# Turning y between the tiles of the norm, weights made early, a final reduce moved ahead and filler products in TensorE's waits

## The chip, the cores and the metric

The kernel runs on one core of a Trainium2 chip. The metric is device time in microseconds of one execution, lower is better. The core has TensorE (PE; its weight loads are shown apart as PEld), VectorE (DVE), ScalarE (ACT), GpSimd (POOL) and SyncE (SP), which here only issues DMA transfers. All engines run their own queue of instructions in order and wait for one another through semaphores. Sixteen DMA engines carry the transfers.

## The reference

The input x is (4, 64, 64, 96): four images, 96 channels. Each image passes a convolution layer with a selective scan, an attention layer and a feed-forward layer, each added to its input; the first works on a group norm (32 groups of three channels over the image). Cut to what matters here:

```python
xz = bilinear(x, W_in, s_in, b_in)            # signs of both operands, 96 -> 384
xp, z = jnp.split(xz, 2, axis=-1)
t = conv3x3(sign(xp + move0), sc * sign(conv_W))   # 192 channels
t = prelu(t + conv_b + rp_b0) + rp_b1 + xp
u = silu(t)                                   # (4, 192, 4096)
# four directions k: rows, columns, and both reversed
dt, B, C = split(bilinear(u_k, Wl, sl, bl));  delta = softplus(bilinear(dt, Wd, sd, bd) + dt_bias)
h = exp(delta * A) * h + delta * u_k * B      # 16 states for each of 192 channels, along 4096 steps
y_k = sum(C * h) + D * u_k
y = y_0 + flip(y_2) + turned(y_1) + turned(flip(y_3))
y = layernorm(y) * ln_w + ln_b;  x = x + bilinear(y * silu(z), W_out, s_out, b_out)
# then linear attention (6 heads, q (k^T v)), and a feed-forward layer in 8-bit floats
```

"Turned" means that rows and columns of the 64 x 64 image are swapped.

## The kernel before

**The scan.** The work is cut into 1536 pieces: 4 images (b) times 4 directions (e, in the order k = 1, 3, 0, 2) times 4 chunks of 1024 steps (ci) times 6 groups of 32 channels (g) times 4 sets of 4 states (q). A piece is a tile of 128 rows (32 channels by 4 states) by 1024 steps. For piece i, `Scans.run` issues in this order: `loads` (broadcasts of B, C and delta, 512 KB each, on SP), `load_sums`, `carry` (the last column of a scan kept for the next chunk, ACT, L1597), `decay` for piece i+1 (exp(delta A) on ACT, L1554), `evacuate` (finished sums of y from PSUM, ACT, L1642), `reduce` for piece i-4 (the sum over states on PE, L1628 and L1633), `inject` for piece i+3 (w = delta u times B, on POOL, recorded at L443), `late_product` and `scan`. The scan itself is one DVE instruction of about 2.3 us; its product with C goes to DVE (1.23 us) or to POOL (2.35 us). Which of them is decided by two running tallies, `c.vec.us` and `c.gps.us`: POOL takes the product if DVE would be later than POOL, and the lead that one has over the other is carried to the next piece, up to 8. All tallied instructions of DVE and POOL carry the line L443.

**What runs beside it.** After each piece, `run` takes one step of the generators in `lanes` (the deltas of later chunks: `prepare`) and one step of `back`. The generator `back` works through everything that is not the scan: the prologues of the next images (projection, convolution, row stage), `turn(c, b)`, and the `Epilogue` of each image, `sums` (norm, gate and output projection of eight tiles of 512 positions), `middle` (the matrix of the attention) and `last` (attention and feed-forward). `turn` takes y of directions 1 and 3, which were scanned by columns, back to rows: sixteen loads yt on SP, sixteen copies yh on ACT (L1015, 96 x 512), and two stores. Direction 2 adds the turned y, so ahead of a piece of direction k = 2 the loop steps `back` until the turn is done:

```python
while KORD[self.pieces[i][1]] == 2 and self.pieces[i][0] not in c.turned:
    next(back)
```

In the kernel before, `back` comes to `turn(c, b+1)` after the sums of image b, or after the last tiles of image b-1. For the third image (b=2) it is this loop that forces it, at pieces 1056 to 1058.

**The head.** Before the first scan, `weights()` makes all constants (signs and transposes of the weights: winT, cwA and cwB, wR for the projection to dt, B and C, wdt, wdz and wdy for delta, sbR its scales, al and anm the decays, woutT and the small ones tpw and tpd). It is a lane that alternates with `prologue(0)`, which has a form of its own for the first image (`alone`): group norm, then `alone_parts`, the convolution in sixteen parts (two halves of 96 channels by eight tiles), and, as the parts leave room, the projection of later tiles (ix and iz, L647 and L648; tp and sz on ACT, L653 and L665). Per part PE makes the products cv (L745), DVE v (L783), ACT r (L784), two or three steps of e (L758, L759, L767) and the sign sg (L722). The signs go out as xg by POOL's queue (L730), a copy ut turned by POOL (L711) goes to memory as utd, and u as ud, by delayed stores on SP (`Later`, L462). Then comes the row stage: xa and xb (L874), their copies xr (L879), the projection acc (L940), tbc (L917) stored as bcd (L952) and the signs sgn (L920) stored as sgd (L953). The signs come back as g (L965), are transposed (gp, L975; gT, L982) and give the first deltas in `start`: dA_s (L1688), two steps w_s and w_d on DVE, and the broadcasts dl_s (L1711). `first_u` loads w_u (L1658, L1660), and `first_loads` loads the eight bc tiles of the first pieces, all on SP.

**The tail.** After the last scan `run` issues `next(back)`, then the last four reduces and the last evacuation (ys). Three lanes then finish the last image's sums: the epilogue's own lane, which has been working beside the scans, and two more (names ln0 and ln1) whose tiles need the last y. A fourth lane (l4) joins for `last`, so eight tiles are done in two rounds of four. In `norm` (products by `mm`, L1143), the form with `alone` set has the mean from PE and subtracts, scales, shifts and gates on DVE; the other form centers by the products yc and scales by the products sy on PE, and has one DVE step g for each half.

Of the kernel before, what the change touches and what calls it, by code (L numbers as in the profile page):

```python
# [25 lines left out]
CH = 1024  # L26
# [27 lines left out]
def hybrid_kernel(ctx: ExitStack, tc: tile.TileContext, a: dict, out: bass.AP):  # L54
# [108 lines left out]
    def weights():  # L163
# [39 lines left out]

        wi = temp("wi", [128, 3, DM], F32)
# [19 lines left out]
        wl = [temp(f"wl{o}", [128, DN], F32) for o in range(2)]  # L224
        for o in range(2):
            nc.gpsimd.memset(wl[o], 0.0)
            for kk in range(2):
                k, r0 = o + 2 * kk, 64 * kk
                nc.sync.dma_start(wl[o][r0 : r0 + 32, :], a["wl_bc"][32 * k : 32 * k + 32, :])
                nc.sync.dma_start(wl[o][r0 + 32 : r0 + 32 + NR, :], a["wl_dt"][k])  # L230
        wd = [temp(f"wd{x}", [128, NK, NR], F32) for x in range(2)]
        nc.sync.dma_start(wd[0], a["wd"][0:128])
        for r0 in (0, 64):
            nc.sync.dma_start(wd[1][r0 : r0 + 64], a["wd"][128:DN])
        wo = temp("wo", [DM, DN], F32)
        nc.sync.dma_start(wo, a["w_out"])
        small = {}
# [22 lines left out]
        nc.vector.tensor_tensor(sbx, pvx[:, :, B_X], pvx[:, :, MOVE0], ALU.add)  # L260
        wim = negmean("wim", wi, DM)
        wis = temp("wis", [128, 3, DM], BF16)
        for t in range(3):
            nc.scalar.activation(wis[:, t, :], wi[:, t, :], AF.Sign, bias=wim[:, t : t + 1])
        ps = transposed(winT, [wis[:, t, :] for t in range(3)])
        for x in range(2):
            nc.vector.tensor_copy(winB[:, 64 * x : 64 * x + 64], ps[0:DM, 128:DN], saturate=False)
        yield
        for i, cut in enumerate(cuts):
            nc.scalar.activation(cwA.rearrange("p t d -> p (t d)")[:, cut], cfa[i], AF.Sign, saturate=False)  # L270
            nc.scalar.activation(cwB[:, lines[i]], cfb[i], AF.Sign, saturate=False)
        yield

        part = temp("part", [96, 2, 2])
        for i in range(2):
            for h in range(2):
                nc.vector.tensor_reduce(part[:, h, i : i + 1], cwn[h][i], AX.X, ALU.add, apply_absolute_value=True)
            yield
# [108 lines left out]
        for name, dst in (("w1", w1q), ("w2", w2q), ("b1", b1q), ("b2", b2q)):  # L387
            q = dst if dst.dtype == F8 else temp(name + "q", list(dst.shape), F8)
            nc.vector.tensor_copy(q, small[name], saturate=False)
            if q is not dst:  # L390
                nc.vector.tensor_copy(dst, q)
# [1448 lines left out]
```

## Time and profile before

| what | us |
|---|---|
| median of three runs | 5361.95 (5360.22 to 5364.72) |
| the profiled execution, and its span | 5356.94, 5355.2 |
| busy: DVE, POOL, ACT, PE | 5004.4, 4951.9, 3606.7, 3387.5 |
| start to first scan | 180.2 |
| first scan to the end of the last | 5055.1 |
| last scan to the end | 120 |

The profile is of one execution. Times are in microseconds, an instruction's name is output<-inputs by the program's names, and L443 and the like are lines of the kernel. In answers in order of time, a line has the start, the duration, the engine, the line and operation, and in square brackets how long the engine was idle before it and what it had waited for last. Lines with an engine's name and q (SPq) are issues of transfers, whose duration is that of the issue alone. In answers by stretch, a line has the stretch, its length, the busy time of PE, PEld, DVE, ACT and POOL, and then the granted clock of TensorE (1 is full), the busy share of the DMA engines and GB/s.

### The profile page before, as it was taken

Reading aid. Unit: us, or ns where it says so; the run is one execution under the profiler, and the core shown is the slowest. Engines: PE = TensorE matmul, PEld = TensorE weight load, DVE = VectorE, ACT = ScalarE, POOL = GpSimd, SP = SyncE. Lnnn points to the kernel's source line nnn. Section 1 sums busy time; section 2 is a strip of 40 time slices with the busy share of each in tenths; the row PEclk is TensorE's granted clock in tenths of the full one; section 3 lists DMA queues with packets and bytes.
Section 4 is the critical chain, followed back from the end, with each engine's and each line's share of the span. In section 5 each row is a group of like instructions: output and inputs, shape, how many; then the busy total and the mean of one; then the engine's idle time right before and its main releaser. Section 6 shows DMA issues by size and latency. Waiting matters only on the chain. (4 is left out here: it accounts for less than half of the span.)

```text
span 5355.2 us, 61897 instructions
## 1 busy us (share of the span) xinstructions
PE 3387.5 (63%) x20029; PEld 1351.6 (25%) x20029; DVE 5004.4 (93%) x3168; ACT 3606.7 (67%) x5644; POOL 4951.9 (92%) x2254
## 2 busy tenths in 40 slices
PE   7457665567645666566676556775666676664577
PEld 3212222122222222222222222222222222221223
DVE  4699999999999999999999999997999999999995
ACT  6577767687766666677777766666776666776554
POOL 4699999999999999999999999998999999999990
PEclk8667776678866877677777768776777776676788
DMA  5666666867766666766666666666666566667652
GB/s 107 189 194 197 212 189 203 260 203 211 222 195 182 205 218 203 230 208 204 216 204 193 193 207 224 195 198 222 201 204 211 189 209 202 200 190 233 217 177 65
DMA packets 605594, 1068.83 MB, mean 200 GB/s; under 512 B 219771, under 2 KB 336916, under 8 KB 603540
## 3 DMA queue, kind: packets, MB, share of 16 engines
q1 hardware_dynamic: 602884, 1063.93, 63.7%
q8 instruction: 157, 2.57, 0.2%
q14 instruction: 169, 1.38, 0.1%
q0 software_dynamic: 1536, 0.79, 0.1%
q10 hardware_dynamic: 848, 0.15, 0.0%
HBM read 829.69 MB, written 228.30 MB: 198 GB/s over the span
## 5 line engine op out<-in xcount | busy, mean ns | idle before, releaser
L443 POOL TENSOR_TENSOR w<-dl,bc 128x1024 f32<-128x1024 f32 x1524 | 3549.5, 2355 | 60.3 <-PE yp L1628 43.7
L1554 ACT ACTIVATE dA<-dl,anm 128x1024 f32<-128x1024 f32 x1524 | 1701.3, 1116 | 511.9 <-DVE w L443 319.0
L443 DVE TENSOR_TENSOR_SCAN dA<-dA,cy,w 128x1024 f32<-128x1024 f32 x726 | 1700.7, 2343 | 61.3 <-ACT dA L1554 50.1
L443 POOL TENSOR_TENSOR w<-h,bc 128x1024 f32<-128x1024 f32 x570 | 1341.4, 2353 | 100.5 <-DVE h L443 95.5
L1628 PE MATMUL yp<-w,sum 128*32 128x256 f32 x12288 | 1230.4, 500 | 157.4 <-ACT pd L1508 109.4
L443 DVE TENSOR_TENSOR w<-dA,bc 128x1024 f32<-128x1024 f32 x966 | 1183.3, 1225 | 63.8 <-DMA bc<-bcd 1.9
L443 DVE TENSOR_TENSOR_SCAN h<-dA,cy,w 128x1024 f32<-128x1024 f32 x426 | 996.8, 2340 | 3.4 <-ACT dA L1554 3.1
L1597 ACT COPY cy<-dA 128x1 f32<-128x1 f32 x723 | 114.2, 158 | 829.1 <-DVE w L443 828.1
L1628 PEld LDWEIGHTS yp<-w,sum 128*32 128x32 f32 x12288 | 320.0, 127 | 1218.4 <-issue 741.0
L443 DVE TENSOR_TENSOR_SCAN dA<-dA,w 128x1024 f32<-128x1024 f32 x240 | 547.7, 2282 | 50.8 <-ACT dA L1554 48.2
L443 DVE TENSOR_TENSOR_SCAN h<-dA,w 128x1024 f32<-128x1024 f32 x144 | 328.1, 2279 | 9.0 <-POOL w L443 8.6
L1489 PE MATMUL dps<-gT,wdz 128*128 128x64 fp8e5 x1008 | 115.5, 314 | 323.8 <-ACT ys L1642 313.8
L1502 PE MATMUL dps<-sp,ident 128*128 128x512 f32 x378 | 266.4, 793 | 73.1 <-ACT dps L1498 72.7
L1633 PE MATMUL yp<-ya,back 128*128 128x256 f32 x576 | 225.6, 511 | 0.0
L1489 PEld LDWEIGHTS <-wdz 128*128 128x128 fp8e5 x1008 | 94.5, 152 | 402.2 <-issue 401.3
L806 PE MATMUL cv<-tp,cwA 128*96 128x512 fp8e5 x432 | 160.2, 492 | 43.1 <-ACT r L838 41.8
L1597 ACT COPY cy<-h 128x1 f32<-128x1 f32 x429 | 79.9, 186 | 158.9 <-DVE h L443 158.6
L1489 PE MATMUL dps<-gT,wdy 128*128 128x64 fp8e5 x504 | 57.0, 312 | 183.1 <-ACT ys L1642 182.8
L1280 PE MATMUL kv<-wkv,tt 97*128 97x192 f32 x240 | 76.8, 491 | 136.9 <-DVE tt L443 136.9
L1494 ACT ACTIVATE pd<-dps,dbias,pvd 128x512 f32<-128x512 f32 x189 | 144.0, 762 | 20.9 <-PE dps L1489 20.6
L1143 PE MATMUL yc<-eys,mean 96*96 96x512 f32 x240 | 133.5, 708 | 35.6 <-DVE vks L443 21.4
L1633 PEld LDWEIGHTS yp<-ya,back 128*128 128x128 f32 x576 | 118.9, 238 | 119.3 <-issue 88.6
(380 smaller groups left out, 4559.2 us busy)
## 6 DMA issues: line engine op xcount, KB each, us to landing
dl<-dld SPq DMA_DIRECT2D x762, 512.0 KB
bc<-bcd SPq DMA_DIRECT2D x512, 512.0 KB
dld<-pd SPq DMA_DIRECT2D x126, 512.0 KB
yd<-ys SPq DMA_DIRECT2D x764, 64.0 KB
dld<-pd SPq DMA_DIRECT2D x126, 256.0 KB
ya<-yd SPq DMA_DIRECT2D x192, 128.0 KB
pu<-ud SPq DMA_DIRECT2D x32, 512.0 KB
pu<-utd SPq DMA_DIRECT2D x31, 512.0 KB
```

The source lines that it names most:

```text
L443: return getattr(self.eng, name)(out, *args, **kw)
L806: nc.tensor.matmul(ps, w[:, 96 * h : 96 * h + 96], tp[:, 8 * q + dy : 8 * q + dy + 8, dx : dx + IW], start=(w is taps[0][1]), stop=(w is t ...
L1143: self.c.nc.tensor.matmul(ps, w, x, start=(i == 0), stop=(i == len(pairs) - 1))
L1280: nc.tensor.matmul(pk[i // 2][:, i % 2], tt[:, 128 * i : 128 * i + 128], c.wkv, start=True, stop=True)
L1489: nc.tensor.matmul(pv[:, s], wd[:, k, s], gT[:, :, c0 : c0 + 16], start=(s == 0), stop=(s == 7))
L1494: nc.scalar.activation(d[:, 0], ps, AF.Abs, scale=sc, bias=bi)
L1502: nc.tensor.matmul(ps, c.ident, t, start=False, stop=True, skip_group_check=True)
L1554: c.nc.scalar.activation(t, self.dlt[i // NQ][0], AF.Exp, scale=c.anm[:, g, NQ * KORD[e] + q : NQ * KORD[e] + q + 1])
L1597: self.c.nc.scalar.copy(self.carries[g, q], h[:, CH - 1 : CH])
L1628: c.nc.tensor.matmul(y[32 * x : 32 * x + 32, g % 2, :], c.sum4, prod[:, 256 * x : 256 * x + 256], start=(q == 0), stop=(q == NQ - 1 and no ...
L1633: c.nc.tensor.matmul(y[:, g % 2, :], w, src, start=False, stop=(n == len(more) - 1))
```

## The change

- `turn(c, b+1)` may now start between two tiles of `sums` or of `last` of image b, as soon as directions 1 and 3 of the next image are scanned (`between`); `back` leaves it out if it was done.
- After the last piece `run` makes no step of `back`, so the last four reduces come first; the tile that the third lane then works on takes the `alone` form of `norm`, with DVE in place of some products on PE.
- `keep_busy` issues products whose result is not used: 8 small ones ahead of the group norm's sums (csum), 24 after the last part of the convolution, 20 after the first image's row stage, and 15 in `middle` and in the first tile of `last` of the last image.
- The loads of wl and wd go to ACT's queue at the start, al is loaded with them; wR and wdt are made before the convolution starts, sbR and al early in it. woutT, tpw and tpd wait until the projection of the first image is over (`c.projected`). wdy's sixteen transfers, `first_u` and the eight first bc loads go to POOL's queue; the bc loads come right after `first_u`, one half of bcd's stores after the signs' stores or after the transposes. `clear_signs` moves ahead of the row stage for the first image.
- The tallies are set to zero after `start`.

```diff
@@ -201,6 +201,17 @@
             nc.vector.tensor_copy(dst, ps[:f, 0:at], saturate=False if dst.dtype == F8 else None)
             return ps

+        wl = [temp(f"wl{o}", [128, DN], F32) for o in range(2)]
+        for o in range(2):
+            nc.gpsimd.memset(wl[o], 0.0)
+            for kk in range(2):
+                k, r0 = o + 2 * kk, 64 * kk
+                nc.scalar.dma_start(wl[o][r0 : r0 + 32, :], a["wl_bc"][32 * k : 32 * k + 32, :])
+                nc.scalar.dma_start(wl[o][r0 + 32 : r0 + 32 + NR, :], a["wl_dt"][k])
+        wd = [temp(f"wd{x}", [128, NK, NR], F32) for x in range(2)]
+        nc.scalar.dma_start(wd[0], a["wd"][0:128])
+        for r0 in (0, 64):
+            nc.scalar.dma_start(wd[1][r0 : r0 + 64], a["wd"][128:DN])
...
-        wo = temp("wo", [DM, DN], F32)
+        wo, al = temp("wo", [DM, DN], F32), temp("al", [128, 2, NK * NS])
         nc.sync.dma_start(wo, a["w_out"])
+        nc.sync.dma_start(al, a["al"].rearrange("p h k s -> p h (k s)"))
         small = {}
...
-            yield
-        nc.vector.tensor_tensor(csc, part[:, :, 0], part[:, :, 1], ALU.add)
-        nc.vector.tensor_scalar(csc, csc, 1.0 / (9 * DN), None, ALU.mult)
-
-        nc.vector.tensor_tensor(cbias, pv[:, :, CONV_B], pv[:, :, RP0], ALU.add)
...
+            nc.scalar.activation(cwB[:, lines[i]], cfb[i], AF.Sign, saturate=False)
+        wdt = [temp(f"wdt{x}", [NR, NK * 32]) for x in range(2)]
+        for x, t in enumerate(wds):
+            transposed(wdt[x].bitcast(F8), [t[:, k, :] for k in range(NK)])
+        yield
...
+            yield
+            if i == 0:
+                for o in range(2):
+                    transposed(wR[:, o].rearrange("p x m -> p (x m)"), [wes[o][:, x, :] for x in range(4)])
+                yield
...
         for r0 in (0, 64):
             for s in range(8):
                 at = r0 + NR * s
-                nc.sync.dma_start(wdy.bitcast(F32)[at : at + NR, :, s, r0 // 4 : r0 // 4 + 16], two[:, :, 0:16])
-        yield
+                nc.gpsimd.dma_start(wdy.bitcast(F32)[at : at + NR, :, s, r0 // 4 : r0 // 4 + 16], two[:, :, 0:16])
+        yield
+        for k in range(NK):
+            o, r0 = k % 2, 64 * (k // 2)
+            nc.sync.dma_start(sbR[r0 : r0 + 32, o, 0:1], a["sl_bc"][0:32, k : k + 1])
+            nc.sync.dma_start(sbR[r0 : r0 + 32, o, 1:2], a["bl_bc"][:, 32 * k : 32 * k + 32].rearrange("o p -> p o"))
+            nc.sync.dma_start(sbR[r0 + 32 : r0 + 32 + NR, o, :], a["sl_dt"][k])
+        al2 = temp("al2", [128, 2, 4, NK * NQ])
+        nc.scalar.activation(al, al, AF.Exp)
+        nc.vector.tensor_scalar(al2, al.rearrange("p h (s j) -> p h j s", j=4), -1.0, None, ALU.mult)
+        yield
+        for g in range(NG):
+            nc.sync.dma_start(anm[:, g, :], al2[32 * (g % 4) : 32 * (g % 4) + 32, g // 4])
         nc.vector.tensor_tensor(dbias, pvd[:, :, NK : 2 * NK], pvd[:, :, 2 * NK :], ALU.add)
         nc.vector.tensor_reduce(dsum, pv[:, :, DSK : DSK + NK], AX.X, ALU.add)
         nc.vector.tensor_reduce(sum4, ident.rearrange("p (d j) -> p d j", j=4), AX.X, ALU.add)
         yield
...
+
+        while not c.projected:
+            yield
+        transposed(woutT.rearrange("p h m -> p (h m)"), [wos[:, 96 * h : 96 * h + 96] for h in range(2)])
         yield
         ps = p.ps.tile([128, 512], F32, name="tpw", tag="y1")
...
     c = SimpleNamespace(**locals())
+    c.projected = False
     c.ready, c.turned, c.later = set(), set(), Later(nc)
     c.vec, c.gps = Tally(nc.vector, 0.15, 1 / 960), Tally(nc.gpsimd, 0.14, 2.16e-3)
     run(c)
@@ -428,6 +432,12 @@
     src = c.a["x"][b].rearrange("(i p) e -> p i e", p=128)
     for q, t in enumerate(xts):
         c.nc.sync.dma_start(t, src[:, 8 * q : 8 * q + 8, :])
+
+
+def keep_busy(c, ps, n):
+
+    for _ in range(n):
+        c.nc.tensor.matmul(ps, c.identb, c.wR[:, 0].rearrange("p x m -> p (x m)"), start=True, stop=True)


 class Tally:
@@ -476,7 +486,9 @@
     made, first = c.weights(), prologue(c, 0, c.xts)
     lanes = [made, first]
     next(made)
-    for _ in range(6):
+    for n in range(6):
+        if n == 4:
+            next(made)
         next(first)
     next(made)
     while (0, 1) not in c.ready:
@@ -503,7 +515,7 @@
             e.open()
             yield from e.sums(e.lane)
             if b + 1 < NB:
-                if scans.done(b + 1, 2, 20):
+                if b + 1 not in c.turned and scans.done(b + 1, 2, 20):
                     while not scans.done(b + 1, 2):
                         yield
                     yield from turn(c, b + 1)
@@ -526,6 +538,7 @@
     more = [e.spare_lane(x) for x in range(2)]
     drain([behind] + [e.sums(ln) for ln in more])
     more.append(e.fourth_lane())
+    c.busy = lambda n: keep_busy(c, more[-1].bank("warm", 1), n)

...
+            if alone:
+                warm = bank("warm", 1)[:, 0:128]
+                for _ in range(8):
+                    nc.tensor.matmul(warm, ident, ident, start=True, stop=True)
             csum = bank("csum", 0)[0:1, 0 : 4 * DM]
...
                                 next(ahead.pop(0), None)
+                                c.projected = not ahead
...
+                        if n == len(parts) - 1:
+                            keep_busy(c, c.p.ps.tile([128, 512], F32, name="warm_cv", tag="y1"), 24)
                         mid = (h, q, pz, v, r, nm)
...
+            def clear_signs():
+                nc.gpsimd.memset(gw[:, :, 0:16], 0.0)
+                nc.gpsimd.memset(gw[:, :, 64:96], 0.0)
+
+            if alone:
+                clear_signs()
...
+                rest = []
...
-                            nc.sync.dma_start(c.bcd[b][k][:, at : at + n], t[r0 : r0 + 32, :])
+                            rest.append((c.bcd[b][k][:, at : at + n], t[r0 : r0 + 32, :]))
                         nc.sync.dma_start(
                             c.sgd[b][k].rearrange("(r l) -> r l", l=L // 4)[:, L // 8 * gh : L // 8 * gh + L // 8],
                             sgw[r0 + 32 : r0 + 32 + NR, :],
                         )
+                    if not (fast and gh):
+                        for pair in rest:
+                            nc.sync.dma_start(*pair)
+                        rest.clear()
                     if fast and gh == 0:
                         c.first_u()
+                        c.loads_ahead()
                     yield
                 c.later.flush()
-                if o:
-                    nc.gpsimd.memset(gw[:, :, 0:16], 0.0)
-                    nc.gpsimd.memset(gw[:, :, 64:96], 0.0)
+                if fast:
+                    keep_busy(c, c.p.ps.tile([128, 512], F32, name="warm_rw", tag="y1"), 20)
+                if o and not alone:
+                    clear_signs()
                 for x, k in enumerate((o, o + 2)):
                     nc.sync.dma_start(gw[:, x, 16:64], c.sgd[b][k].rearrange("(p f) -> p f", p=128))
-                    if fast and x:
-                        c.loads_ahead()
                     yield
                     yield
...
+                        for pair in rest:
+                            nc.sync.dma_start(*pair)
                         continue
...
     def sums(self, ln):
         c, nxt = self.c, None
         while nxt is not None or self.todo or not self.opened:
+            if ln is self.lane:
+                yield from self.between()
             q, nxt = nxt, None
...
+    def between(self):
+
+        b = self.b + 1
+        if not self.alone and b < NB and b not in self.c.turned and self.scans.done(b, 2):
+            yield from turn(self.c, b)
+
...
+        busy = c.busy if self.alone else lambda n: None
+        busy(4)
         (c.vec if self.alone else c.gps).tensor_tensor(m0, self.vks, c.hmask, ALU.mult)
         ps = ln.bank("m1", 1)[0:96, 0:96]
         mm(ps, [(m0, c.wff)])
+        busy(2)
         yield
         nc.scalar.copy(m1, ps)
         ps = ln.bank("m2", 0)[0 : DM + 1, 0:96]
         mm(ps, [(c.wqT, m1)])
+        busy(2)
         yield
         c.vec.tensor_tensor(m2, ps, c.bff, ALU.add)

@@ -1335,6 +1382,7 @@
...
         while nxt:
+            yield from self.between()
...
                 mm(ps, [(self.ms[2], tt)])
+                if ln is self.lane and n == 1:
+                    c.busy(4)
...
+            if self.alone and ln is self.lane and n == 1:
+                c.busy(3)
...
-    def load_bc(self, w, to, b, e, ci, q):
+    def load_bc(self, w, to, b, e, ci, q, eng=None):
         c = self.c
         t = c.p.bc.tile([128, CH], F32, name=f"bc{w}_{b}_{e}_{ci}_{q}", tag=f"bc{w}")
         src = c.bcd[b][KORD[e], 16 * w + 4 * q : 16 * w + 4 * q + 4, CH * ci : CH * ci + CH]
-        c.nc.sync.dma_start(t, src.unsqueeze(0).to_broadcast([32, 4, CH]))
+        (eng or c.nc.sync).dma_start(t, src.unsqueeze(0).to_broadcast([32, 4, CH]))
...
-        nc.sync.dma_start(v[0], ud[0:128, 0:16])
+        nc.gpsimd.dma_start(v[0], ud[0:128, 0:16])
         for x in range(2):
-            nc.sync.dma_start(v[1][64 * x : 64 * x + 64, 0:8], ud[128:DN, 8 * x : 8 * x + 8])
+            nc.gpsimd.dma_start(v[1][64 * x : 64 * x + 64, 0:8], ud[128:DN, 8 * x : 8 * x + 8])

...
-        for w, to in enumerate((self.bt, self.ct)):
-            for q in range(NQ):
-                self.load_bc(w, to, 0, 0, 0, q)
+        for w, q in ((0, 0), (1, 0), (0, 1), (0, 2), (0, 3), (1, 1), (1, 2), (1, 3)):
+            self.load_bc(w, (self.bt, self.ct)[w], 0, 0, 0, q, self.c.nc.gpsimd)
...
             pass
+        c.vec.us = c.gps.us = 0.0
         self.decay(0)
         for i in range(AHEAD):
             self.inject(i)
...
-            next(back, None)
+            if i < n - 1:
+                next(back, None)
         self.late_product()
         for i in range(n - 4, n):
             self.reduce(i)
```

## The prediction

> **What bounds the kernel now.** I read the totals first, then equal stretches of the span, then the head and the tail instruction by instruction.
>
> ```profile
> PE 3387.5 (63%) x20029; PEld 1351.6 (25%) x20029; DVE 5004.4 (93%) x3168; ACT 3606.7 (67%) x5644; POOL 4951.9 (92%) x2254
> ...
> DVE  4699999999999999999999999997999999999995
> ```
>
> DVE and POOL share the scans and products and are full except in the head, the tail and the slice that shows 7. The first scan starts at 180.2 us, the last ends at 5235.3, and 120 us follow. Between them only a wait of DVE or POOL costs time. Stretches of 96 pieces, by engine in the order PE, PEld, DVE, ACT, POOL, then clock, DMA share, GB/s:
>
> ```profile
> 503.40:818.60 315.20, 212.14 (x1289) 81.28 (x1289) 303.60 (x182) 229.53 (x357) 304.27 (x132) 0.75 0.66 201
> 3648.80:3983.30 334.50, 206.60 (x1172) 84.28 (x1172) 302.07 (x179) 233.81 (x367) 303.24 (x133) 0.72 0.67 212
> 3983.30:4297.00 313.70, 199.58 (x1116) 77.83 (x1114) 308.32 (x194) 196.08 (x312) 309.72 (x136) 0.76 0.62 199
> ```
>
> The sixteen stretches take 311 to 317 us (mean 314) except the second one here, at 334.5 with no more work in it. The order of time shows why, on DVE and then on ACT:
>
> ```profile
> 3679.14 2.30 DVE L443 TENSOR_TENSOR_SCAN dA<-dA,w 128x1024 f32<-128x1024 f32 x1 [23.96 <-ACT dA L1554]
> ...
> 3659.38 2.03 ACT L1015 COPY yh<-yt 96x512 f32<-96x512 f32 x2 [4.40 <-DMA yt<-yd]
> 3670.24 7.72 ACT L1015 COPY yh<-yt 96x512 f32<-96x512 f32 x8 [8.83 <-DMA yt<-yd]
> ```
>
> ACT stands in the forced turn of y (b=2), its copies waiting 14.1 us in all for transfers, and the next decay (L1554) is queued behind them. In the head, ACT and SP, then SP, PE and DVE:
>
> ```profile
> 93.28 0.31 ACT L402 ACTIVATE slab<-slab 128x128 f32<-128x128 f32 x1 [7.14 <-DMA slab<-in_al]
> ...
> 91.48 0.35 SPq L400 DMA_DIRECT2D slab<-in_al  x1
> ```
> ```profile
> 148.81 0.86 SPq L1658 DMA_DIRECT2D w_u<-utd  x1
> ...
> 156.86 5.67 SPq L1520 DMA_DIRECT2D bc<-bcd  x8
> ...
> 157.65 1.03 PE L975 MATMUL gp<-ident,g 128*128 128x128 fp8e5 x8 [11.30 <-DMA g<-sgd]
> ...
> 178.84 1.23 DVE L443 TENSOR_TENSOR w<-dl_s,bc 128x1024 f32<-128x1024 f32 x1 [8.59 <-DMA dl_s<-w_s]
> ...
> 191.50 2.29 DVE L443 TENSOR_TENSOR_SCAN h<-dA,w 128x1024 f32<-128x1024 f32 x1 [6.28 <-POOL w L443]
> ```
>
> The load of al was issued last in a row of small ones; g came 11.3 us late; the first product waited for dl_s while eight bc loads shared the DMA engines (share 0.98 at 286 GB/s from 157.7 to 180.2). In the tail, PE and then two stretches:
>
> ```profile
> 5236.83 6.85 PE L1143 MATMUL yc<-eys,mean 96*96 96x512 f32 x8 [2.86 <-DVE vks L443]
> 5243.61 1.93 PE L1628 MATMUL yp<-w,sum 128*32 128x256 f32 x32
> ```
> ```profile
> 5287.00:5311.00 24.00, 21.49 (x28) 5.83 (x29) 8.07 (x15) 9.84 (x16) 0.00 (x0) 0.51 0.23 66
> 5311.00:5335.00 24.00, 19.78 (x92) 10.47 (x90) 15.72 (x31) 17.06 (x29) 0.00 (x0) 0.99 0.12 33
> ```
>
> The last sums of y stand behind 6.85 us of another tile's cold centering, and the last stage starts 24 us at half clock.
>
> [...] fv took 2.02 us in the 0.51 stretch, 1.10 after it. [...] convolution products here take 216 ns. [...] the trace has only 16 KB transfers there:
>
> ```profile
> 131.75 1.47 POOL L730 DMA_DIRECT2D xg<-sg  x3 [1.27 <-ACT sg L722]
> ```
>
> **The turn.** By the two instruction orders, b=2's sixteen copies move from pieces 1056–1058 (fourteen at 1058, forced) to 976–995, b=3's from 1407–1426 to 1359–1378; b=0 and b=1 stay at their 238–257 and 593–612, whose stretches show no such wait. Sixteen copies of 1.07 us still run, in ACT's slack (67% busy). Five tiles and the next middle come about 20 pieces later and end well before the last batch. So the stretch falls from 334.5 to 314: −20.5 us (at best −24, the whole wait; at worst −17).
>
> **Head.** (1) The loads of wl, wd and al and the preparation of wR and wdt move ahead of the convolution; ix (L647) then waits for two more wR copies, and behind it on PE stand every projection and the convolution, for which ACT's tp and DVE's v wait: +2.5. ACT now issues the eleven loads of wl and wd; SP took 0.31 to 0.85 us for each small one above, so some 4 us, before ACT's first sign has its data: 0, at worst +3. The sbR, al and anm issues come ahead of SP's stores of u, whose queue has room there: 0. (2) The convolution advances part by part with v (L783), from 36.8 to 128.2. With projection a part needs some 4.6 us (ACT's two kinds, 4.14 and 5.06), without it 3.7. Freed of al's 7.14 and of the weights' slots between parts: 39.3 + 11×4.6 + 4×3.7 = 104.7, plus the two waits of u for a store (3.25 each), = 111: −17, including (1). Bounds: −9 if the utd stores (64-byte runs, some 11 us a pair) now limit it, −21. (3) Row stage, with signs cleared earlier: −1. (4) w_u leaves SP (1.99 us) and bcd goes behind sgd (1.5 of its 1.82 us), so g comes 3.5 earlier; its second half stands behind four bcd issues, +1. (5) Eight bc issues (5.67 us) leave SP and start ahead of g; the bytes are the same, so I take half of the 8.59 wait for dl_s, −4.5 (0 to −8.6). (6) Sixteen wdy loads go to POOL, which waits 42 us for dl_s later: 0, at worst +2. (7) 24 fillers after the convolution cost 24×0.216 = 5.2 us while PE waits for row data (0.16 us busy of 7.5); the 20 at the row stage cost 8.6 cold or 4.3 warm in a wait of some 8, but must wait until the last evacuation frees their bank, and gp is queued behind them on PE, for which dA_s and the first product wait: +1 (−1 to +4). The woutT, tpw and tpd products, held back until projection is over, fit in PE's gaps between the last four parts: 0, at worst +1. The 8 f32 ones ahead of csum fall in PE's wait: 0. Sum −17 −1 −2.5 −4.5 +1 = −24: first scan at about 156.
>
> **Start.** With both tallies at zero, ten first products go to DVE instead of POOL's queue, net four more: the waits of 6.28 and 2.32 go, 4×1.23 comes: −3.7 (−1 to −6).
>
> **Tail.** The guard on the last step puts the final reduce ahead of the third lane's centering: −6.85 on ys. That tile then runs the other form beside two lanes: four yc and four sy products fewer, two mu more, twelve DVE operations at 0.65 to 0.74 (8.4 us) in a DVE busy 18.5 of 51.6: +1. Fillers: 15×0.216 = 3.2 us, in PE's waits around m (0.78, 0.32, 0.35, 0.78, 0.68), so about 1 shows. If they hold the clock, the first round of outputs (31.3 us, from 5285.2 to 5316.5) approaches the second (25.9): −5.4. Sum −11 (−15 if all hides; −3 if the clock still falls and fillers delay).
>
> **Sum.** −24 −3.7 −20.5 −11 = −59.2 against the profiled 5356.9 gives 5297.7. The median shown is 5.0 above that execution; on it, 5361.95 − 59.2 = 5302.8: 5303. About 0.2% (10.7 us) is what a measurement can tell from no change.
>
> **Rivals.** A: the head stays bound by transfers. For it: DMA share 0.79 to 0.98 from 128 to 180. Against: 0.45 in the convolution. Head −10, time 5317. B: the turn's wait only moves, because yt also waits at its new place, or tail fillers land on the path: it gives back 16 to 20, time about 5321. Against: b=0 and b=1 are turned likewise without it. C, slower: the software queue is slow. By bytes, POOL moves 16 KB per 0.49 us, 33 GB/s; w_u and eight bc (5.24 MB) would take 157 us from about 135, and the fourth piece needs them all by 191: ready at 292, +101. Less the 35 from turn, start and tail: 5428. It decides where the queue takes over 91 us, below 58 GB/s. Against: if the price is per descriptor (32 in 0.49 us), 128 take 2 us[...]. D: a part that does not act: fillers too short to lift the clock, tail −6: 5308, inside the likeliest range.
>
> **How the numbers follow.** Likeliest 0.67 (D within it), A 0.18, B 0.09, C 0.05, and 0.01 for none. Own range of the likeliest: 5288 to 5318, its unknowns (head 8, tail 5, turn 3) not all adding. Taking in A and most of B: 5282 to 5328, leaving out C, the worst of B and the tails. Faster 0.93, same 0.01, slower 0.06.
>
> **What would show it.** Right: first scan near 156; v's last part near 111 with no al wait; no stretch over 318; no 24 us wait of DVE; last product to end about 109; clock over 0.8 in the first 24 us of the last stage. Wrong: bc landings on POOL's queue over 10 us each; u waiting for utd stores; first product waiting for bc; fillers on PE ahead of gp or of fc with PE's successors waiting.

## The result and the profile after

The changed kernel takes 5302.12 us (median of 4 runs, 5301.18 to 5303.59) against 5361.09 us for the kernel before beside it (median of 4, 5360.19 to 5364.72). The ratio is 0.9889, with a 95% interval of 0.9872 to 0.9906. The forecast was 5303 us. The profiled execution has a span of 5300.1 us, 55.1 less than before. It falls into three parts:

| part | before | after | difference | forecast |
|---|---|---|---|---|
| start to first scan | 180.2 | 161.2 | −19.0 | −24 |
| first scan to the end of the last | 5055.1 | 5034.4 | −20.8 | −20.5 −3.7 = −24.2 |
| end of the last scan to the end | 119.9 | 104.5 | −15.3 | −11 |
| span | 5355.2 | 5300.1 | −55.1 | −59.2 |

The median fell by 59.0 and the profiled spans by 55.1, because the execution profiled before was one of the quicker ones of its kernel. Over the 27 executions of the kernel before that were measured beside the experiments, the median is 5359.43, which makes the fall 57.3. So the forecast's nearness to the median is in part luck: of its four terms three were too large and one too small, and the median that it started from, 5361.95, was 2.5 above that of the 27.

The totals of the profile page of the kernel after, in the form shown for before (engine, busy us, share, instructions; then DVE's busy tenths in 40 slices). Line numbers have moved with the edit; what was L443 is L453 here:

```profile
PE 3359.1 (63%) x20089; PEld 1345.6 (25%) x20092; DVE 5011.8 (95%) x3178; ACT 3610.2 (68%) x5644; POOL 4957.2 (94%) x2277
...
DVE  5799999999999999999999999999999999999996
```

DVE and POOL have as much to do as before (7.4 and 5.3 us more); the 7 in the middle is gone. The stretches of 96 pieces of the kernel after, first an ordinary one, then pieces 1056 to 1151 and the next:

```profile
481.50:795.10 313.60, 210.37 (x1289) 81.01 (x1289) 303.54 (x182) 229.75 (x357) 304.52 (x132) 0.77 0.66 202
3628.00:3944.20 316.20, 211.07 (x1197) 86.37 (x1191) 304.12 (x183) 215.68 (x346) 306.25 (x135) 0.75 0.67 210
3944.20:4258.20 314.00, 205.28 (x1116) 78.01 (x1115) 306.40 (x189) 202.18 (x324) 308.00 (x136) 0.73 0.61 194
```

The stretch that took 334.5 takes 316.2, with about the same DVE work (304.1 against 302.1). The sixteen copies yh of the third image now lie one by one between 3361.8 and 3421.4, and ACT waited for yt ahead of none of them. The head after the convolution, in order of time, on SP, then PE, then DVE:

```profile
130.68 0.35 SPq L1000 DMA_DIRECT2D g<-sgd  x1
131.12 1.88 SPq L1020 DMA_DIRECT2D bcd<-tbc  x4
133.10 0.63 SPq L1000 DMA_DIRECT2D g<-sgd  x1
...
149.41 13.16 SPq L1762 DMA_DIRECT2D dl_s<-w_s  x6
```
```profile
136.66 0.62 PE L1008 MATMUL gp<-ident,g 128*128 128x128 fp8e5 x8 [2.21 <-DMA g<-sgd]
141.10 0.61 PE L1008 MATMUL gp<-ident,g 128*128 128x128 fp8e5 x4 [3.82 <-DMA g<-sgd]
```
```profile
159.83 1.23 DVE L453 TENSOR_TENSOR w<-dl_s,bc 128x1024 f32<-128x1024 f32 x1 [7.95 <-DMA dl_s<-w_s]
161.16 2.30 DVE L453 TENSOR_TENSOR_SCAN dA<-dA,w 128x1024 f32<-128x1024 f32 x1
```

The convolution's last v starts at 109.3 (128.2 before). From there to the first scan it is 51.9 us, where it was 52.0: all of the head's gain was made before v's last part, and what was changed behind it gave nothing on balance. The second g took 8 us from its issue to its use. The eight bc loads landed 7.5 to 13.9 us after their issues. In the tail, PE and then a stretch of the last stage:

```profile
5197.47 1.13 PE L1685 MATMUL yp<-ya,back 128*128 128x256 f32 x4
5198.44 1.88 PE L1178 MATMUL mu<-eys,on 96*96 96x512 f32 x4
```
```profile
5239.00:5263.00 24.00, 20.06 (x68) 7.98 (x68) 14.00 (x27) 15.82 (x27) 0.00 (x0) 1.00 0.31 91
```

The last sums come ahead of the third lane's tile, and the first 24 us of the last stage, which ran at clock 0.51, now run at 1.00.

### The profile page after: what moved, and what is told of

Same layout as the page of the kernel before. It is cut to its first block, busy times and chain, and to the rows that moved or that the text cites. A ratio compares the mean times of both kernels' runs of the same rounds, so it can differ in the third digit from the quotient of the medians.

```text
span 5300.1 us, 62028 instructions
## 1 busy us (share of the span) xinstructions
PE 3359.1 (63%) x20089; PEld 1345.6 (25%) x20092; DVE 5011.8 (95%) x3178; ACT 3610.2 (68%) x5644; POOL 4957.2 (94%) x2277
## 5 line engine op out<-in xcount | busy, mean ns | idle before, releaser
L453 POOL TENSOR_TENSOR w<-dl,bc 128x1024 f32<-128x1024 f32 x1524 | 3550.7, 2357 | 44.8 <-PE yp L1680 31.1
L453 DVE TENSOR_TENSOR_SCAN dA<-dA,cy,w 128x1024 f32<-128x1024 f32 x726 | 1700.8, 2343 | 60.6 <-ACT dA L1606 44.5
L453 POOL TENSOR_TENSOR w<-h,bc 128x1024 f32<-128x1024 f32 x566 | 1333.7, 2356 | 102.5 <-DVE h L453 94.8
L1680 PE MATMUL yp<-w,sum 128*32 128x256 f32 x12288 | 1215.8, 494 | 151.6 <-ACT pd L1560 102.4
L453 DVE TENSOR_TENSOR w<-dA,bc 128x1024 f32<-128x1024 f32 x970 | 1188.1, 1225 | 70.1 <-DMA bc<-bcd 9.1
L453 DVE TENSOR_TENSOR_SCAN h<-dA,cy,w 128x1024 f32<-128x1024 f32 x426 | 996.9, 2340 | 3.8 <-ACT dA L1606 3.4
L453 DVE TENSOR_TENSOR_SCAN dA<-dA,w 128x1024 f32<-128x1024 f32 x244 | 556.9, 2282 | 23.9 <-ACT dA L1606 21.2
L453 DVE TENSOR_TENSOR_SCAN h<-dA,w 128x1024 f32<-128x1024 f32 x140 | 319.0, 2278 | 0.3 <-ACT dA L1606 0.3
L1178 PE MATMUL sy<-eys,meanw 96*96 96x512 f32 x232 | 139.1, 737 | 36.4 <-ACT eys L1263 36.4
L1547 ACT ACTIVATE sp<-dps,dbias,pvd 128x512 f32<-128x512 f32 x189 | 144.9, 767 | 0.0
```

Source lines behind the costliest of these rows:

```text
L453: return getattr(self.eng, name)(out, *args, **kw)
L1178: self.c.nc.tensor.matmul(ps, w, x, start=(i == 0), stop=(i == len(pairs) - 1))
L1547: nc.scalar.activation(t, ps, AF.Relu, scale=sc, bias=bi)
L1680: c.nc.tensor.matmul(y[32 * x : 32 * x + 32, g % 2, :], c.sum4, prod[:, 256 * x : 256 * x + 256], start=(q == 0), stop=(q == NQ - 1 and no ...
```

## Experiments

All times are medians, of four executions each where no other number is given; twelve kernels were run. The kernel before had medians of 5358 to 5361 us beside them. Figures of a trace, first scans and tails among them, are of one execution. Executions of the same head differ by some us: with the head as changed and untouched, the first scan came at 159.8, 159.8, 160.3, 160.5, 161.2 and 163.0 in six kernels. The scans together scatter too: 5031 to 5040 us in eight kernels with the new turn and zeroed tallies, 5053 to 5057 in three with the old ones.

**The turn, undone.** The changed kernel with the turn at its old places:

```diff
-            if ln is self.lane:
-                yield from self.between()
...
-                if b + 1 not in c.turned and scans.done(b + 1, 2, 20):
+                if scans.done(b + 1, 2, 20):
...
         while nxt:
-            yield from self.between()
```

> The changed kernel with the turn of y back at its old places (no turn between tiles). My theory: the turn between tiles is worth the wait of DVE at the forced turn of the third image, some 18 to 20 us and nothing else: the stretch of pieces 1056 to 1151 goes from 316 back to about 334, a wait of DVE of about 24 us returns near it, first scan (161) and tail (105) stay, time 5302 + 19 = 5321. Rival: the gain was not that wait but the later work of the last images being spread differently, so that the stretch comes back to 334 but others shrink: time 5302 to 5310.

Measured: 5327.09 us, ratio to before 0.9935 (0.992 to 0.995); first scan 159.8, tail 104.1. The wait is back, on DVE of this kernel:

```profile
3664.95 2.30 DVE L453 TENSOR_TENSOR_SCAN dA<-dA,w 128x1024 f32<-128x1024 f32 x1 [23.86 <-ACT dA L1603]
```

The stretch takes 335.6 again (+19.4). The median is 25.0 above the changed kernel's and the scans together took 24.9 more; most of the rest lies in the stretch ahead of it, at 321.2 against 313.7. So the wait itself is what the theory said; the sum was above it, and why that stretch grew is open.

**The turn, alone.** The kernel before with `between`, its two calls and the guard in `back` that leaves out a turn already done, and nothing else:

```diff
-                if scans.done(b + 1, 2, 20):
+                if b + 1 not in c.turned and scans.done(b + 1, 2, 20):
...
+            if ln is self.lane:
+                yield from self.between()
...
         while nxt:
+            yield from self.between()
```

> The kernel before with the turn between tiles alone, nothing else changed. Theory: first scan 180 and tail 120 as before, the wait of 24 us at the forced turn of the third image goes, the stretch of pieces 1056 to 1151 falls to 314 to 317, the scans together by 18 to 25 us; time 5337 to 5341. Rival: part of what undoing it cost (25 us, with one neighbouring stretch 7 us longer) was scatter: the scans fall by 13 to 17 us only, time 5343 to 5347.

Measured: 5344.66 us (8 executions), ratio 0.9973 (0.9962 to 0.9983), 14.8 us less. The rival's figure came, but not for the rival's reason. Stretches of this kernel, pieces 1056 to 1151 and then 1152 to 1343:

```profile
3649.80:3964.50 314.70, 213.60 (x1198) 86.73 (x1191) 304.23 (x184) 215.29 (x346) 306.27 (x134) 0.74 0.66 211
3964.50:4602.60 638.10, 423.88 (x2279) 163.20 (x2279) 613.62 (x379) 403.20 (x641) 616.02 (x270) 0.74 0.60 195
```

and of the kernel before, pieces 1152 to 1343:

```profile
3983.30:4612.20 628.90, 408.80 (x2266) 155.84 (x2265) 614.93 (x382) 401.20 (x639) 618.58 (x271) 0.74 0.62 201
```

The stretch of pieces 1056 to 1151 loses 19.8 us (334.5 to 314.7), and the next two give back 9.2 us with no more work on DVE or POOL. What DVE waited for there, in us, times and longest, first in the kernel before, then with the turn alone:

```profile
DVE pd L443 <- PE dps L1502: 0.5, 1, 0.5
```
```profile
DVE pd L443 <- PE dps L1511: 9.3, 5, 3.2
```

One such wait, in the order of time of the kernel with the step after the last piece as before (its run is told below), PE twice and then DVE:

```profile
4205.02 7.11 PE L1178 MATMUL yc<-eys,mean 96*96 96x512 f32 x8 [0.64 <-DVE vks L453]
...
4212.63 1.12 PE L1554 MATMUL dps<-sp,ident 128*128 128x512 f32 x2
...
4213.79 0.69 DVE L453 TENSOR_TENSOR pd<-dps,pu 128x512 f32<-128x512 f32 x1 [3.04 <-PE dps L1554]
```

The turn between tiles shifts five tiles of the second image and all of the third by 16 to 22 pieces; in their new place the four yc products of a tile (eight instructions) stand on PE just ahead of the delta's transposition dps. Where they ran cold, that is mostly at half clock, DVE waited for dps: here 3.04 us behind 7.11 us of yc. Over the ten kernels with the new turn (this one among them) these two stretches took 628.5 to 638.1, mean 633, against 627 to 629 in the four with the old one: of the 20 us, about 5 are given back. In the changed kernel's profiled execution this happened to be nothing (628.5, with 3.0 us of such waits). The clock tells why. A tile's yc on PE and the pd behind it on DVE, in that execution, around piece 1216:

```profile
4151.28 3.67 PE L1178 MATMUL yc<-eys,mean 96*96 96x512 f32 x8 [1.02 <-DVE vks L453]
...
4158.19 0.68 DVE L453 TENSOR_TENSOR pd<-dps,pu 128x512 f32<-128x512 f32 x1
```

Here the clock was full, and pd did not wait. In the kernel quoted above the same tile's yc took 6.92 us at a mean clock of 0.53, and pd waited 1.59. With the new turn the waits come at the same five tiles (near pieces 1216, 1232, 1248, 1280 and 1296). In the kernel with the turn alone all five ran at least partly cold (5.4 to 7.1 us) and pd waited each time (1.3 to 3.2); in the changed kernel's execution two ran so (5.5 and 5.4 us, 1.4 of wait each), and at the other three pd waited 0.2 us at most. In the kernel before, cold yc products stand in another place and cost DVE 0.5 us at most. So what the new places cost depends on when the clock is low, which differs from trace to trace.

**The tail's fillers, left out.** All fifteen filler products in `middle` and `last`, the calls of `busy`, are removed (their results are used by nothing).

```diff
-        busy(4)
         (c.vec if self.alone else c.gps).tensor_tensor(m0, self.vks, c.hmask, ALU.mult)
...
-        busy(2)
...
-        busy(2)
...
-                if ln is self.lane and n == 1:
-                    c.busy(4)
...
-            if self.alone and ln is self.lane and n == 1:
-                c.busy(3)
```

> The changed kernel without the 15 filler products of the tail. Theory: they keep TensorE's clock at full through the last stage; without them the clock falls to 0.5 to 0.6 for some 24 us there and the tail grows from 104.6 by 4 to 6 us, time 5307. Rival 1: the earlier final reduce packs PE's work so closely that the clock stays up by itself: tail 103 to 105, time 5302. Rival 2: as theory, but the third lane's form matters more, tail +1 to +2.

Measured: 5316.84 us, ratio 0.9915 (0.990 to 0.993), tail 117.6: 13.1 us more, over twice the theory's. Two stretches of this kernel's last stage:

```profile
5243.60:5263.60 20.00, 17.04 (x22) 4.49 (x23) 6.07 (x11) 7.17 (x12) 0.00 (x0) 0.56 0.31 90
5263.60:5283.60 20.00, 19.65 (x51) 10.05 (x50) 10.84 (x23) 10.61 (x18) 0.00 (x0) 0.50 0.08 22
```

The clock fell at 5246.0 and stayed at half until 5283.5, for 37.5 us, though PE was busy for 19.65 of the last 20 us. In the kernel before, and in the three kernels made from it, the same stage was cold for 23.9 us each time.

**The fillers of the last stage only.** The eight around m are removed, the seven of the first tile stay:

```diff
-        busy(4)
...
-        busy(2)
...
-        busy(2)
```

> The changed kernel with only the seven tail fillers of the first tile of the last stage; the eight around m are left out. Without all fifteen the clock was at half for some 36 us and the tail took 117.6 instead of 104.6. Theory: the low activity around m (1.2 us of products in 3 us) is what lets the clock fall, so the seven that follow come too late [...]: tail 108 to 118, time 5306 to 5315. Rival: seven products in the waits of at, fc and fv are enough: tail 104 to 106, time 5302.

Measured: 5302.64 us, ratio 0.9895 (0.9881 to 0.991), tail 104.1. The rival holds: seven products, 1.8 us in all, behind the products at and fc are enough. The clock in the 24 us from 5236 was 1.00.

**The step after the last piece, as before.**

```diff
-            if i < n - 1:
-                next(back, None)
+            next(back, None)
```

> The changed kernel with the step of the back work after the last piece as before, so that the third lane's centering stands ahead of the last four reduces again. Theory: the last sums of y come 6 to 7 us later after the last scan, and the lanes with them: tail 110 to 112, time 5308 to 5310. Rival: another chain sets the end (the two lanes hide it, or the other form of the norm costs what the order gives): tail 103 to 106, time 5301 to 5304.

Measured: 5311.74 us, ratio 0.9908 (0.9891 to 0.9925), tail 110.8, as the theory said. PE of this kernel:

```profile
5202.28 6.82 PE L1178 MATMUL yc<-eys,mean 96*96 96x512 f32 x8 [2.80 <-DVE vks L453]
5209.03 1.93 PE L1680 MATMUL yp<-w,sum 128*32 128x256 f32 x32
```

The four combinations are now measured. Split at the first product at, which opens the last stage, the tails are, in us:

| kernel | last scan to at | at to the end | tail |
|---|---|---|---|
| neither part (the kernel before) | 49.9 | 70.0 | 119.9 |
| the early reduce alone (no tail fillers) | 43.1 | 74.5 | 117.6 |
| the fillers alone (the step as before) | 49.8 | 61.0 | 110.8 |
| both (the changed kernel) | 43.5 | 61.0 | 104.5 |

Ahead of at, the early reduce is worth 6.3 to 6.7 us either way. Behind it, the fillers are worth 9.0 with the old order and 13.5 with the new, because without them the clock stayed at half for 23.9 us in the one case and 37.5 in the other. That is one trace of the latter; why it was longer is open.

**The first loads, back on SP.** w_u and the eight bc loads are issued by SP, the latter behind the second g load and in their old order:

```diff
-        nc.gpsimd.dma_start(v[0], ud[0:128, 0:16])
+        nc.sync.dma_start(v[0], ud[0:128, 0:16])
...
-                        c.loads_ahead()
...
+                    if fast and x:
+                        c.loads_ahead()
```

> The changed kernel with w_u and the eight first bc loads back on SP, the bc loads behind the second g load and in their old order; the rest of the head as changed. Theory after the result: their early start on the other queue gained nothing, because their bytes run beside the second g load (8 us from its issue to its use) and the first dl_s are limited by their own transfer: first scan 158 to 162, time 5299 to 5303. Rival, my prediction's step: moving them is worth 4 to 5 us: first scan 165 to 166, time 5307.

Measured: 5305.49 us, ratio 0.9897 (0.9882 to 0.9911), first scan 161.0: no gain from the other queue. PE and DVE of this kernel show the exchange:

```profile
138.48 0.61 PE L1009 MATMUL gp<-ident,g 128*128 128x128 fp8e5 x4 [1.80 <-DMA g<-sgd]
```
```profile
159.65 1.23 DVE L453 TENSOR_TENSOR w<-dl_s,bc 128x1024 f32<-128x1024 f32 x1 [10.39 <-DMA dl_s<-w_s]
```

The second gp comes 2.6 us earlier than in the changed kernel and the wait for dl_s is 2.4 longer. In these two traces the bytes of bc seem to delay either the one or the other. The 3.4 us in the median are not in the head; they are in the scans (5038.4) and within their scatter.

**Both g loads first.** The second g load goes ahead of the four bcd stores, and six of the eight bc loads follow the first pair of dl_s:

```diff
+                    if fast and x:
+                        for pair in rest:
+                            nc.sync.dma_start(*pair)
...
-                        for pair in rest:
-                            nc.sync.dma_start(*pair)
                         continue
...
-        for w, q in ((0, 0), (1, 0), (0, 1), (0, 2), (0, 3), (1, 1), (1, 2), (1, 3)):
+        for w, q in ((0, 0), (1, 0)):
             self.load_bc(w, (self.bt, self.ct)[w], 0, 0, 0, q, self.c.nc.gpsimd)
...
             self.dlt[n] = pair
+            if n == 0:
+                self.more_loads()
```

> The changed kernel with the second g load issued ahead of the four stores of bcd, and of the eight first bc loads only two issued before it; the other six follow the first pair of dl_s. Theory: the second g (8 us from issue to use among other transfers) holds up the product gp on PE, and dA_s behind it, so the first scan comes 3 to 5 us earlier, at 156 to 158; the six late loads then cost some of it in the first pieces, so the start of piece 96 (481.5) moves by 0 to -4; time 5299 to 5303. Rival: the first scan is held by the transfer of dl_s alone whatever is ahead of it: first scan 160 to 162, and the late loads cost 3 to 8 us: time 5306.

Measured: 5299.53 us, ratio 0.989 (0.9875 to 0.9904). PE and DVE:

```profile
137.32 0.40 PE L1011 MATMUL gp<-ident,g 128*128 128x128 fp8e5 x4 [1.02 <-DMA g<-sgd]
```
```profile
155.53 2.30 DVE L453 TENSOR_TENSOR_SCAN dA<-dA,w 128x1024 f32<-128x1024 f32 x1
```

The first scan is 5.6 us earlier than in the changed kernel, outside the scatter of six, and piece 96 starts at 477.2 instead of 481.5. The kernel with both edits, told last, has it early too (156.3). So the transfers around g did hold the head; the edit moved both g and six bc loads, and doesn't tell them apart. Against a scatter of a few us, 2.6 in the median is no proof of a faster kernel.

**No fillers in the head.** The 8, 24 and 20 products are removed (unused results).

```diff
-            if alone:
-                warm = bank("warm", 1)[:, 0:128]
-                for _ in range(8):
-                    nc.tensor.matmul(warm, ident, ident, start=True, stop=True)
...
-                            keep_busy(c, c.p.ps.tile([128, 512], F32, name="warm_cv", tag="y1"), 24)
...
-                    keep_busy(c, c.p.ps.tile([128, 512], F32, name="warm_rw", tag="y1"), 20)
```

> The changed kernel without the filler products of the head (8, 24 and 20). Theory: they lie in TensorE's waits; [...] the first scan is 0 to 3 us later (161 to 164), time 5302 to 5305. Rival: the 20 at the row stage hold gp back and cost: first scan 1 to 4 us earlier, 157 to 160, time 5299.

Measured: 5298.9 us, ratio 0.989 (0.9875 to 0.9904); first v 41.0 (41.2 to 42.7 in the six with the same head), first scan 159.5, just under the six. The rival's figures came, but its reason did not: in the changed kernel PE had finished the 20 fillers and stood idle for 2.21 us ahead of gp, waiting for g, as the line of gp above shows. Neither a gain nor a loss can be told: the head's fillers are worth nothing that shows.

**The tallies, not zeroed.**

```diff
-        c.vec.us = c.gps.us = 0.0
         self.decay(0)
```

> The changed kernel without the zeroed tallies after the start. Theory: the first products go to POOL again, DVE waits for the injected w of the third and fourth piece for 6.3 and 2.3 us, so the first 96 pieces take 323 to 324 instead of 320.4, first scan unchanged at 161, time 5304 to 5306. Rival: within what the stretches scatter (3 us), no difference: 5301 to 5303.

Measured: 5314.25 us, ratio 0.9919 (0.9902 to 0.9936). DVE at the start:

```profile
171.12 2.29 DVE L453 TENSOR_TENSOR_SCAN h<-dA,w 128x1024 f32<-128x1024 f32 x1 [6.29 <-POOL w L453]
175.74 2.29 DVE L453 TENSOR_TENSOR_SCAN h<-dA,w 128x1024 f32<-128x1024 f32 x1 [2.32 <-POOL w L453]
```

Both waits are back, and the first 96 pieces take 323.3 us instead of 320.4: +2.9, as the theory said. The median is 12 higher, of which the profile (span 5306.6) shows these 3 and some 5 more in the scans behind. Nearly all of those lie in pieces 1152 to 1343 (634.4 against 628.5), where kernels with the new turn scatter about 633. The rest stays open.

**The wait for al alone, twice.** In the kernel before, the loads of al and sbR are moved to the start of the head; then al's alone:

```diff
         nc.sync.dma_start(wo, a["w_out"])
+        al = temp("al", [128, 2, NK * NS])
+        nc.sync.dma_start(al, a["al"].rearrange("p h k s -> p h (k s)"))
...
-        al, al2 = temp("al", [128, 2, NK * NS]), temp("al2", [128, 2, 4, NK * NQ])
-        nc.sync.dma_start(al, a["al"].rearrange("p h k s -> p h (k s)"))
+        al2 = temp("al2", [128, 2, 4, NK * NQ])
```

> The kernel before with one edit: the loads of al and of sbR moved from the convolution to the start of the head, their uses where they were. Theory: ACT's wait of 7.1 us for al goes, and nothing else of the convolution's gain, so the last v comes at 121 instead of 128, the first scan at 173 instead of 180, time 5354 against 5361. Rival: the convolution's gain of the changed kernel is mostly this wait (queues behind SP's row of small loads too): last v at 112 to 116, first scan 164 to 168, time 5346.

Measured: 5358.6 us (12 executions), ratio 1.0003 (0.9994 to 1.0011). POOL's clearing of sbR now waited 27 us for the loads, and so did everything behind it: the first v came at 46.0 instead of 36.8. The sum tells of that placing, not of al. From first to last v it took 83.1 us instead of 91.4, with no wait for a store in al's place.

> The kernel before with one edit: the load of al at the start of the head, sbR's loads left where they were (with sbR moved as well, the clearing of sbR on POOL waited for its loads and delayed the convolution's start by 9 us). Theory: ACT's wait of 7.1 us goes and the convolution from its first v to its last takes 83 to 84 us instead of 91.4, with its start unmoved at 37: last v at 120 to 121, first scan 172 to 173, time 5353. Rival: stores or the weights' slots take its place: last v 124 to 128, first scan 176 to 180.

Measured: 5355.57 us (20 executions), ratio 0.9992 (0.9985 to 0.9999); first v 36.4, last v 124.8, first scan 175.5. The wait for al is gone (v's eighth part at 86.2 instead of 93.8), and 4.3 of the 7.6 us are given back, as the rival said. DVE and SP of this kernel:

```profile
111.07 0.69 DVE L444 TENSOR_TENSOR u<-cz,e 96x512 f32<-96x512 f32 x1 [4.09 <-DMA ud<-u]
```
```profile
98.70 3.91 SPq L463 DMA_DIRECT2D utd<-ut  x1
102.70 5.24 SPq L463 DMA_DIRECT2D ud<-u  x1
```

The parts run into the stores of u, which SP's issues of utd and ud had held for 9 us. The wait for al alone is thus worth 3.3 us at the last v. Where the rest of the convolution's 24 us comes from, the traces show by part: from the first to the eighth v the kernel before took 57.0 us and the changed one 30.6. Of these 26.4 us, 7.6 are al's. Also between these parts, the kernel before has DVE's copies of transposed weights (wR, slab, woutT and meanw), ahead of which DVE waited 15 us for PE; the changed kernel has none of these copies there. From the eighth to the sixteenth v, where woutT, tpw and tpd now lie, it took 36.5 instead of 34.4. The weights' slots were not moved alone in any run.

**Both head edits together.** Both g loads first, five bc loads early and three late, no head fillers:

```diff
-        for w, q in ((0, 0), (1, 0), (0, 1), (0, 2), (0, 3), (1, 1), (1, 2), (1, 3)):
+        for w, q in ((0, 0), (1, 0), (0, 1), (0, 2), (1, 1)):
...
+        for w, q in ((0, 3), (1, 2), (1, 3)):
+            self.load_bc(w, (self.bt, self.ct)[w], 0, 0, 0, q, self.c.nc.sync)
```

> The changed kernel with both g loads ahead of the stores of bcd, five of the eight first bc loads early and three after the first pair of dl_s, and no filler products in the head. Theory: the two gains add in the head, first scan 153 to 156, the start of piece 96 at 475 to 477, tail as changed: time 5295 to 5298. Rival: without the fillers' warm clock the earlier g gains less: first scan 157 to 159, time 5299 to 5302.

Measured: 5299.65 us, ratio 0.9888 (0.9872 to 0.9905); first scan 156.3, piece 96 at 477.1. They don't add; it is as good as the earlier g alone, and the time is the rival's. By the medians it is 2.5 us better than the changed kernel, less than these measurements can tell.

## Why the prediction was right, and where not

**The turn (−20.5).** The mechanism was right: done alone or undone, the wait of 24 us goes and comes with it, and the stretch moves by 19.4 to 19.8 us (18.2 in the changed kernel's own trace). What failed is the step "five tiles and the next middle come about 20 pieces later", which was costed at nothing. Over the kernels with the new turn it costs about 5 us in pieces 1152 to 1343, on PE, an engine that is busy 63% of the time, so the term comes to about −15. Done alone, the turn gained 14.8; undoing it lost 25.0, with some of that in a stretch where no cost was expected. The size is known no better than these two figures.

**The head (−24, measured −19.0).** Two steps erred and partly cancelled. Ahead of the convolution I had +2.5; the first v came 5.5 us later (42.3 against 36.8). That is step (1): the first ix started at 30.45 instead of 24.01. ACT, which now issued the loads of wl and wd and made their signs, took up the group norm's sums (csr) at 15.19 instead of 13.12, a term put at 0 (at worst +3); and ix then waited 3.3 us for the copies of wR. From first to last v I had some 72 us (111 less 39.3); it took 67.0. Of this the parts were right, 65.4 in the sum against 66.0, and the two waits of u of 3.25 us were not: in the kernel before u waited for a store for 0.71 and 3.25, and the second lies behind the last v, at 133.95. In the changed kernel one of 1.0 came. The last v at 109.3 instead of 111 is the sum. Behind it I had −7 and measured nothing. That is steps (4) and (5): sgd's last issue did come 6 to 7 us earlier in relation to the last v, but w_u, five bc loads and four bcd stores then ran beside the two g loads, and the second, which dA_s does not read, stands on PE ahead of dA_s: gT was ready at 138.3, and dA_s began at 141.9. The step failed in counting SP's issue time and not the transfers in flight; the run with the loads back on SP, with its first scan at 161.0 against 161.2, shows it. No bc load on POOL's queue had been measured, only transfers of 16 KB; the first bc landed 7.5 us after its issue, and the eight together took from 130.9 to 150.6. Five of them took more than 10 us, which I had named as a sign of being wrong. Rival C's price by bytes (157 us for w_u and bc) is ruled out by the same figures. Rival A was half right: the convolution was not held by transfers, but the part behind it stayed so, as the run with both g loads first shows; it took 51.9 us, and 52.0 before.

**The start (−3.7).** Right in place and nearly in size: 2.9 by the first 96 pieces (the median of the run without it was 12 higher, most of which is open). In the kernel before that stretch took 323.2 us; my "311 to 317" for all stretches but one had left it out.

**The tail (−11, measured −15.3).** The reduce's share (−6.85 + 1) was right: 6.3. The fillers' was mis-sized: I took the second round of outputs (25.9 us) as the warm floor for the first. At full clock the first output came 22.7 us after the product at (5239.0 to 5261.7), not 25.9, against 31.4 before: −8.7 in place of −5.4. The whole stage behind at shrank by 9.0. The sum was also off by itself: with the 1 us that the fillers were to show, its terms give −10.3.

**What it rests on.** Against the profiled execution the sum was off by 4.1 us: errors of +5.0 (head), +3.4 (scans) and −4.3 (tail) met. The range from 5282 to 5328 was as wide as these asked for. So most of the places were right, and the closeness of the sum is in good part luck.

## What to carry to other kernels

A generator's work that is forced at its deadline can be moved to where its data are ready, but the work that it displaces lands somewhere too (here it gave back about 5 of 20 us): after such a move, look at the engines that are not the bound in the stretches behind it. Moving the first loads to another queue moved their issue, not their bytes, and the first scan stayed (161.2 on POOL's queue, 161.0 on SP's); with both g loads ahead and six bc loads later it came at 155.5. So order transfers by who needs them first, across all queues. Filler products paid here where they bridge a sparse spot ahead of a long dense stage (the tail took 104.5 with them, 117.6 without), and seven were enough (104.1); in the head's waits they paid nothing that could be told (first scan 161.2 with them, 159.5 without).

## What was not expected of the hardware

For the run without tail fillers some 24 us at half clock were expected; it was 37.5. In the last 20 us of these PE was busy for 19.65, and the clock stayed at 0.50 all the same. In the kernel before it was 23.9 us, with PE busy 21.5 of 24. (Busy means that products ran, not how much each of them did.) That the fillers would lift or hold the clock was an estimate of mine. With the seven bf16 products of the last stage alone, issued 0.22 us apart, the clock was 1.00 in the 24 us from 5236; with all fifteen it was 1.00 in the 51 us from 5239, over the same work of the stage. In the traces of the kernels before and after, each of the clock's records (594 and 560) says either full or half, and each but the last, which the end cuts off, is a multiple of 3.41 us long (the 23.9 are seven of them). What makes the clock fall or come back was not shown.
